# Gates of the last nine blocks of nodes as diagonal matrices on TensorE, and a bias added one stage later

## The chip, the cores and the metric

The kernel runs on one core of one Trainium2 chip. The metric is the device time of one execution in microseconds. Engines are named as the profile names them: PE is TensorE (PEld its weight loads), DVE is VectorE, ACT is ScalarE, POOL is GpSimd and SP is SyncE, which only issues DMAs here.

## The reference

Four layers work on one table of 6250 nodes with 256 features, `x`. Each adds its result to `x`, and each begins with a layer norm of `x` without learned weights. The two in the middle meet in the change:

```python
def _L0_ffn_ref(x, ...):                  # the second layer: attention gates, four experts
    ...
    scores = _layernorm(agg, ln_gamma, ln_beta).reshape(M, HEADS, NUM_EXPERTS).mean(1)
    topk_s, topk_i = jax.lax.top_k(scores, TOP_K)
    w = jax.nn.softmax(topk_s, axis=-1)
    out = jnp.zeros_like(x)
    for ei in range(NUM_EXPERTS):
        g = jnp.where(topk_i == ei, w, 0.0).sum(-1)
        hh = jax.nn.gelu(x @ W1[ei] + b1[ei], approximate=False)
        out = out + g[..., None] * (hh @ W2[ei] + b2[ei])
    return out

def _L1_gnn_ref(x, edge_vals, Wp, bp, W1, b1, W2, b2, src, dst):     # the third layer
    h = jax.nn.relu(x @ Wp.T + bp)
    msgs = edge_vals[:, None] * (h ** 2)[src]
    agg = jax.ops.segment_sum(msgs, dst, num_segments=N) ** 0.5
    return h @ W1.T + b1 + agg @ W2.T + b2

x = x + _L0_ffn_ref(_layernorm(x)[None], ...)[0]
x = x + _L1_gnn_ref(_layernorm(x), edge_weight, ...)
x = x + _L1_ffn_ref(_layernorm(x)[None], ...)[0]
```

So each node's four expert outputs are weighted by the node's own four gates (two of them zero), summed and added to `x`. The third layer adds `b1 + b2`, the same row for every node, to its result.

## The kernel before

**Tiling.** The nodes lie in T = 49 blocks of P = 128 (the last holds 106). `x_all` holds the whole of `x` in SBUF, one block as 128 partitions by 256 elements; `b_all`, of the same shape, holds what the next product reads. Everything is f32.

**The second layer.** Three things run interleaved. POOL gathers edges and the attention sums (`add_up`, `score`, `weigh`, `spread_out`) run over 80 groups. The generator `experts1` (L1571) computes the experts' outputs in units of one expert and two blocks, in batches of eight blocks (the last batch, blocks 40 to 48, has nine; within a batch all units of expert 0 come first, those of expert 3 last). A unit makes `hh` by two products and a Gelu (L1607), then `py` = `hh` times `W2` in PSUM, adds the bias into `ys` (L1623), and SP stores `ys` to `y1_dram` (L1627). The generator `gates` (L1845) turns the attention sums of some blocks into `gate[:, w, e]`, for blocks up to 8, 16, 24, 32, 36, 40, 44 and 49; the last two calls thus cover blocks 40 to 43 and 44 to 48.

**The sums and the table for the next layer.** `load_outputs` (L1934) loads a block's four outputs back from `y1_dram` as soon as all four are stored and a buffer of `y1` is free (eight buffers, two blocks). `node_values` (L1945) takes two blocks at a time (the last pass one, block 48). On DVE it adds the four outputs, each multiplied by its gate, to `x_all` (L1952: `x_all = y * gate + x_all`, the gate one value per partition), and takes mean and variance (L1957 to L1959). ACT makes the square root (L1963), DVE the reciprocal and the offset (L1965, L1966), ACT the normalized block `xn` (L1972), PE transposes it (L1982), ACT copies it into `b_all` (L1983), PE multiplies by `wpt` and ACT applies the bias and Relu (L1989). PE transposes back (L1993), ACT squares into `hp` (L1995), and SP stores `hp` to `hp_dram` (L1996). All these PSUM tiles, and those of the experts' `py`, share one name, `py`, with two buffers.

**The third and fourth layers.** When all 49 blocks of `hp_dram` are stored, POOL gathers rows of it, one instruction (L1104) for 128 edges, 831 in all, four groups of six ahead. For each, DVE makes the weights `eq` (L2390) and PE adds up `pe` (L2411), which first is set to zero by a product with the tile `nothing` (L2406). When a group of blocks is complete (four, two or one block), `roots` (L2419) adds `b12` = `b1 + b2` to these blocks of `x_all` on DVE (L2422) and takes the square root of `pe` on ACT (L2428). `end_of2` then makes for every block the two products with `w1t` and `w2t` in PSUM (`pm`), adds them to `x_all` on DVE (L2229) and begins the last layer norm (L2231 to L2236, L2238 to L2242). The gates and experts of the fourth layer (`gates2`, `experts2`) follow, and the result is stored.

**What sets the order.** Each engine runs its instructions in order. The order on an engine is not that of the text: instructions that depend on little stand earlier. The adds of L2422, in the text behind the first gathers, run from 2456.38, before any gather; the products of L2406 run at 2451.49, ahead of the last transposes of `node_values`.

Of the kernel before, what the change touches and what calls it, by code (L numbers as in the profile page):

```python
# [8 lines left out]
F32 = mybir.dt.float32  # L9
I32 = mybir.dt.int32  # L10
AF = mybir.ActivationFunctionType
OP = mybir.AluOpType
# [4 lines left out]
P = 128  # L17
# [824 lines left out]
def kernel(ctx: ExitStack, tc: tile.TileContext, a: dict, out: bass.AP):  # L842
# [10 lines left out]
    N, D = a["x"].shape  # L853
    T = -(-N // P)
# [23 lines left out]
    H, X = a["L0_ffn_att_src"].shape  # L878
# [21 lines left out]
    V, SC, TE, GP, SY = nc.vector, nc.scalar, nc.tensor, nc.gpsimd, nc.sync  # L900
# [16 lines left out]
    with ExitStack() as fast:  # L917
# [4 lines left out]
        ident = const.tile([P, P], F32, name="ident")  # L922
# [43 lines left out]
        if T1 > C1:  # L966
            V.memset(flat.bitcast(I32)[:, C1:T1], 2**24)
            n = E1 - C1 * P
# [52 lines left out]
        x_all = const.tile([P, T, D], F32, name="x_all")  # L1021
# [66 lines left out]
        def mm(dst, lhs, rhs, n=2):  # L1088

            for c in range(n):  # L1090
                TE.matmul(dst, lhs(c), rhs(c), start=c == 0, stop=c == n - 1)  # L1091
# [91 lines left out]
        gate = att.tile([P, T, X], F32, name="gate")  # L1183
# [96 lines left out]
        with ExitStack() as layer:  # L1280
# [29 lines left out]
            with (  # L1310
# [16 lines left out]
                for t0, t1 in parts0:  # L1327
                    b = t0 // TB
# [5 lines left out]
                    for i in range(t1 - t0):  # L1334
# [4 lines left out]
                            scale=rs[:, i : i + 1],  # L1339
# [224 lines left out]
        psy = experts.enter_context(tc.tile_pool(name="py5", bufs=2, space=PSUM))  # L1564
# [85 lines left out]
        def advance(queue, n):  # L1650
            for _ in range(n):
                if queue and next(queue[0], queue) is queue:
                    queue.pop(0)

        layers = [experts1()]
        part = sums.tile([P, 3, T, H], BF16, name="part")
        with (
# [273 lines left out]
            ys = {}  # L1931
# [13 lines left out]
            def node_values(ws):  # L1945

                mv = n6.tile([P, 2, 2], F32, name="ln_mv")
                rs = n6.tile([P, 2], F32, name="ln_rs")
                off = n6.tile([P, 2], F32, name="off")
                for i, w in enumerate(ws):  # L1950
                    for e in range(X):
                        V.scalar_tensor_tensor(  # L1952
                            x_all[:, w, :], ys.pop((w, e)), gate[:, w, e : e + 1], x_all[:, w, :],
                            op0=OP.mult, op1=OP.add,
                        )
                    st = n6.tile([P, 6], F32, name="ln_st")
                    V.bn_stats(st, x_all[:, w, :])  # L1957
                    V.bn_aggr(mv[:, i, :], st)
                    V.tensor_scalar(rs[:, i : i + 1], mv[:, i, 1:2], EPS, None, op0=OP.add)  # L1959
                    done["sums"] += 1  # L1960
                    yield w == ws[-1]
                n = len(ws)
                SC.activation(rs[:, 0:n], rs[:, 0:n], AF.Sqrt)  # L1963
                yield False
                V.reciprocal(rs[:, 0:n], rs[:, 0:n])  # L1965
                V.scalar_tensor_tensor(  # L1966
                    off[:, 0:n], mv[:, 0:n, 0], -1.0, rs[:, 0:n], op0=OP.mult, op1=OP.mult
                )
                xns = {}
                for i, w in enumerate(ws):  # L1970
                    xns[w] = n6.tile([P, D], F32, name="xn")
                    SC.activation(  # L1972
                        xns[w], x_all[:, w, :], AF.Identity, bias=off[:, i : i + 1],
                        scale=rs[:, i : i + 1],
                    )
                    yield False
                begun.remove(ws)
                for w in ws:
                    pt = psy.tile([P, 2, D], F32, name="py")[:, 0, :]
                    for c in range(2):  # L1980
                        at = slice(c * P, (c + 1) * P)
                        TE.transpose(pt[:, at], xns[w][:, at], ident)  # L1982
                    SC.activation(b_all[:, w, :], pt, AF.Copy)  # L1983
                    yield False
                for w in ws:
                    ph = psy.tile([P, 2, D], F32, name="py")[:, 0, 0:P]
                    mm(ph, lambda c: wpt[:, c, :], lambda c: b_all[:, w, c * P : (c + 1) * P])

                    SC.activation(b_all[:, w, 0:P], ph, AF.Relu, bias=bp)  # L1989
                    yield False  # L1990
                for w in ws:
                    py = psy.tile([P, 2, D], F32, name="py")
                    TE.transpose(py[:, 0, 0:P], b_all[:, w, 0:P], ident)  # L1993
                    hp = n6.tile([P, PD], F32, name="hp")
                    SC.activation(hp, py[:, 0, 0:P], AF.Square)  # L1995
                    SY.dma_start(nodes(hp_dram)[:, w, :], hp)  # L1996
                    yield False
# [157 lines left out]
        blocks = [(t, BT) for t in range(0, small, BT)]  # L2155
        blocks += [(t, 2) for t in range(small, T - 3, 2)] + [(t, 1) for t in range(T - 3, T)]
        with (
# [62 lines left out]
            def end_of2(b, i, root):  # L2220


                w = blocks[b][0] + i
                pm = psm.tile([P, D], F32, name="pt")
                mm(
                    pm, lambda c: (b_all[:, w, 0:P], root[:, i, :])[c],
                    lambda c: (w1t, w2t)[c],
                )
                V.tensor_add(x_all[:, w, :], x_all[:, w, :], pm)  # L2229
                st = wk.tile([P, 6], F32, name="ln_st")  # L2230
                V.bn_stats(st, x_all[:, w, :])  # L2231
                mv = wk.tile([P, 2], F32, name="ln_mv")
                V.bn_aggr(mv, st)
                rs = wk.tile([P, 1], F32, name="ln_rs")
                V.tensor_scalar(rs, mv[:, 1:2], EPS, None, op0=OP.add)
                SC.activation(rs, rs, AF.Sqrt)  # L2236
                yield
                V.reciprocal(rs, rs)  # L2238
                off = wk.tile([P, 1], F32, name="off")
                V.tensor_scalar(off, mv[:, 0:1], rs, -1.0, op0=OP.mult, op1=OP.mult)  # L2240
                xn = wk.tile([P, D], F32, name="xn")
                SC.activation(xn, x_all[:, w, :], AF.Identity, bias=off, scale=rs)  # L2242
                yield
                transposed(psm, b_all[:, w, :], xn)
                yield
                pg = psm.tile([P, D], F32, name="pt")
                mm(pg[:, 0:NX], lambda c: b_all[:, w, c * P : (c + 1) * P], lambda c: gw[:, c, :])
                V.tensor_add(logits(b)[:, i * NX : (i + 1) * NX], pg[:, 0:NX], gb)
# [169 lines left out]

            def roots(b):  # L2419
                n = blocks[b][1]  # L2420
                at = slice(blocks[b][0], blocks[b][0] + n)
                V.tensor_add(  # L2422
                    x_all[:, at, :], x_all[:, at, :],
                    b12[:, None, :].to_broadcast([P, n, D]),
                )
                root = wk.tile([P, BT, P], F32, name="gt")[:, 0:n, :]
                pe = sums.pop(b)[:, 0 : n * P].rearrange("p (w k) -> p w k", k=P)
                SC.activation(root, pe, AF.Sqrt)  # L2428
                return [(b, i, root) for i in range(n)]
# [116 lines left out]
```

## Time and profile before

| What | us |
|---|---|
| median of 3 runs (3552.38 to 3555.68) | 3555.01 |
| the profiled execution, its own time | 3555.79 |
| its span (what the profile covers) | 3554.0 |
| gates of blocks 40 to 43 ready (end of L1921) | 2426.9 |
| gates of blocks 44 to 48 ready (end of L1921) | 2441.1 |
| last store of experts' outputs issued (L1627) | 2444.2 |
| sums and statistics of block 48 done (L1959) | 2454.2 |
| last store to `hp_dram` issued (L1996) | 2464.7 |
| first gather of the third layer (L1104) | 2467.6 |
| last of the 831 gathers starts | 3505.4 |
| last DVE instruction | 3545.3 |

The times below the span count from its start. Over the span PE is busy 94%, DVE 61%, ACT 40% and POOL 63%; these are means over stages with different limits, and the change acts in a short part of one stage and all along another. Two lines show the groups of instructions that the change removes or moves (by their durations; the second line has six smaller ones besides):

```profile
L1952 DVE SCALAR_TENSOR_TENSOR x_all<-y,gate,x_all x196: 446/477/503, 1716.8 to 2452.9; 128x256 f32<-128x256 f32 x196
L2422 DVE TENSOR_TENSOR x_all<-x_all,b 128x1024 f32<-128x1024 f32 x10 | 11.7, 1219 | 0.0
```

The first reads: smallest, median and largest duration in ns, then the starts of the first and the last. The second: total us, mean ns of one, and the idle time of the engine ahead of them. The six smaller ones are 128x512 (three) and 128x256 (three); the six together take 3.3 us.

### The profile page before, as it was taken

Reading aid. Unit: us, or ns where it says so; the run is one execution under the profiler, and the core shown is the slowest. Engines: PE = TensorE matmul, PEld = TensorE weight load, DVE = VectorE, ACT = ScalarE, POOL = GpSimd, SP = SyncE. Lnnn points to the kernel's source line nnn. Section 1 sums busy time; section 2 is a strip of 40 time slices with the busy share of each in tenths; the row PEclk is TensorE's granted clock in tenths of the full one; section 3 lists DMA queues with packets and bytes.
Section 4 is the critical chain, followed back from the end, with each engine's and each line's share of the span. In section 5 each row is a group of like instructions: output and inputs, shape, how many; then the busy total and the mean of one; then the engine's idle time right before and its main releaser. Section 6 shows DMA issues by size and latency. Waiting matters only on the chain.

```text
span 3554.0 us, 57573 instructions
## 1 busy us (share of the span) xinstructions
PE 3338.9 (94%) x20063; PEld 2662.0 (75%) x20063; DVE 2170.1 (61%) x6210; ACT 1412.1 (40%) x2750; POOL 2252.3 (63%) x2367
## 2 busy tenths in 40 slices
PE   7999999999999999999999999997678988989898
PEld 3577777777777778888888888895456666666677
DVE  9999996444544444787758576977234444444464
ACT  4444444444444444444544454664011212211133
POOL 0376666666666664676656555662777777777773
PEclk9999999999999999999999999998567776777797
DMA  6456656656555554433434343553112222222221
GB/s 174 128 189 189 184 183 184 186 186 182 183 183 188 181 183 142 110 97 96 125 88 127 83 130 84 154 94 109 52 53 59 60 59 59 59 59 60 65 62 37
DMA packets 342928, 428.52 MB, mean 121 GB/s; under 512 B 139174, under 2 KB 246453, under 8 KB 342630
## 3 DMA queue, kind: packets, MB, share of 16 engines
q1 hardware_dynamic: 245174, 244.98, 22.1%
q0 software_dynamic: 89408, 178.08, 19.4%
q8 instruction: 162, 2.65, 0.3%
q10 hardware_dynamic: 8048, 1.68, 0.2%
q14 instruction: 136, 1.11, 0.1%
HBM read 382.05 MB, written 42.49 MB: 119 GB/s over the span
## 4 chain that ended last, share of the span: by engine, by line
PE 66%; POOL 14%; DMA 7%; issue 7%; DVE 4%; ACT 1%; SPq 0%; ACTq 0%; POOLq 0%; DVEq 0%
PE ph L1091 32%; POOL hg L1104 13%; PE py L1091 10%; PE pt L1085 7%; PE pe L1443 6%; PE po L1771 5%; DMA hg<-hp_dram,src 5%; PE pt L1091 2%; DMA rb<-low_dram 1%; PE pe L2411 1%; PE pa L1708 1%; PE pm L1091 1%; DVE junk L982 1%; DVE key L1240 0%; DVE order L1237 0%
## 5 line engine op out<-in xcount | busy, mean ns | idle before, releaser
L1104 POOL DMA_INDIRECT yg<-y_dram,src x882 | 847.0, 960 | 543.1 <-issue 226.7
L1104 POOL DMA_INDIRECT hg<-hp_dram,src x831 | 785.7, 946 | 269.2 <-issue 224.3
L1104 POOL DMA_INDIRECT sg<-gat_dram,src x640 | 614.1, 960 | 350.1 <-issue 161.5
L1091 PE MATMUL ph<-w1b,et 128*128 128x256 f32 x3528 | 835.7, 380 | 0.0
L1091 PEld LDWEIGHTS ph<-w1b,et 128*128 128x128 f32 x3528 | 637.0, 190 | 68.7
L2411 PE MATMUL pe<-eq,hg 128*128 128x96 f32 (+15 forms) x2036 | 439.9, 353 | 148.9 <-DMA hg<-hp_dram,src 120.6
L2411 PEld LDWEIGHTS pe<-eq,hg 128*128 128x128 f32 x2036 | 388.2, 260 | 251.8 <-issue 94.6
L1417 DVE TENSOR_TENSOR yg<-ph,yg 128x512 f32<-128x512 f32 x441 | 303.3, 688 | 375.3 <-PE ph L1091 370.7
L2390 DVE TENSOR_SCALAR eq<-px,dst,ew 128x96 f32<-128x96 f32 x831 | 262.0, 370 | 217.2 <-PE pe L2411 120.6
L1091 PE MATMUL ph<-b_all,w 128*128 128x256 f32 (+1 forms) x1600 | 387.1, 380 | 1.5 <-ACT hh L1607 1.4
L1091 PE MATMUL py<-w,hh 128*128 128x256 f32 x1568 | 383.1, 384 | 5.0 <-ACT hh L1607 4.5
L1086 ACT ACTIVATE et<-pt 128x512 f32<-128x512 f32 x441 | 262.2, 596 | 254.4 <-PE pt L1085 242.1
L1422 ACT ACTIVATE h<-yg 128x512 f32<-128x512 f32 x441 | 276.1, 626 | 215.4 <-DVE yg L1417 209.0
L1091 PEld LDWEIGHTS py<-w,hh 128*128 128x128 f32 x1568 | 288.7, 190 | 41.2 <-ACT hh L1607 6.6
L1091 PEld LDWEIGHTS ph<-b_all,w 128*128 128x128 f32 x1600 | 290.0, 190 | 33.7 <-ACT hh L1607 2.0
L1607 ACT ACTIVATE hh<-ph,b 128x256 f32<-128x256 f32 (+1 forms) x400 | 166.7, 467 | 285.6 <-PE ph L1091 279.7
L1085 PE MATMUL pt<-ident,ea 128*128 128x128 f32 x1764 | 272.1, 277 | 3.4 <-ACT et L1086 3.4
L1085 PEld LDWEIGHTS pt<-ident,ea 128*128 128x128 f32 x1764 | 210.2, 144 | 65.0 <-issue 40.4
L1771 PE MATMUL po<-pp,B 128*128 128x240 f32 (+10 forms) x1280 | 252.1, 337 | 2.2 <-DVE acc L1777 2.1
L1771 PEld LDWEIGHTS po<-pp,B 128*128 128x128 f32 x1280 | 215.6, 190 | 14.3 <-DVE acc L1777 2.8
L1443 PE MATMUL pe<-h,eq 128*32 128x257 f32 x3168 | 216.8, 384 | 3.7 <-ACT h L1422 1.9
L1443 PEld LDWEIGHTS pe<-h,eq 128*32 128x32 f32 x3168 | 96.2, 109 | 102.6 <-issue 35.0
(330 smaller groups left out, 4264.5 us busy)
## 6 DMA issues: line engine op xcount, KB each, us to landing
ea<-in_edge_attr_dram SPq DMA_DIRECT2D x147, 768.0 KB
y<-y SPq DMA_DIRECT2D x196, 128.0 KB
w<-in_L_ffn_W_dram SPq DMA_DIRECT2D x48, 512.0 KB
y<-ys SPq DMA_DIRECT2D x96, 256.0 KB
rb<-low_dram SPq DMA_DIRECT2D x80, 256.0 KB
yg<-y_dram,src POOLq DMA_INDIRECT x882
hg<-hp_dram,src POOLq DMA_INDIRECT x831
sg<-gat_dram,src POOLq DMA_INDIRECT x640
```

The source lines that it names most:

```text
L982: V.tensor_scalar(junk, flat, float(w * P), None, op0=OP.is_lt, op1=OP.add, accum_out=below[:, w : w + 1],)
L1085: TE.transpose(pt[:, c, :], src[:, c * P : (c + 1) * P], ident)
L1086: SC.activation(dst, pt.rearrange("p c k -> p (c k)"), AF.Copy)
L1091: TE.matmul(dst, lhs(c), rhs(c), start=c == 0, stop=c == n - 1)
L1104: GP.indirect_dma_start(out=dst, out_offset=None, in_=table[0:NP, :], in_offset=IndirectOffsetOnAxis(ap=idx, axis=0),)
L1417: V.tensor_add(y, ph, y)
L1422: SC.activation(h[:, j : j + 2, 0:D], y, AF.Relu)
L1443: TE.matmul(sums[w][b * Q : (b + 1) * Q, :], eq[k][:, j, at], h[:, i * NT + j, :], start=g == 0 and j == NT - 1, stop=g == last_of[b] and ...
L1607: SC.activation(hidden[u][:, f, :n, :], ph[:, f - f0, :n, :], AF.Gelu, bias=b1[:, e, f : f + 1],)
L1771: TE.matmul(po.rearrange("p b v -> p (b v)"), B[:, j, :], pp[:, j, 0:n, :].rearrange("p b v -> p (b v)"), start=half == 0 and j == 0, stop ...
L2390: V.tensor_scalar(equals[k][:, j, :], lanes[:, 0:NW], dst_of[:, t : t + 1], ew[:, t : t + 1], op0=OP.is_equal, op1=OP.mult,)
L2411: TE.matmul(sums[b][:, lo - t0 * P : hi - t0 * P], hg[:, j, :], eq[:, j, lo - n0 : hi - n0], start=False, stop=after >= (t0 + n) * P,)
```

## The change

For the last nine blocks (40 to 48) the four products on DVE go. Instead ACT multiplies the identity matrix by a block's gates, one expert at a time, which gives four diagonal matrices of 128x128 in a new tile `dg` (one buffer, 2 KB in each partition); PE multiplies each diagonal by the expert's output and sums the four in a PSUM tile of the name `py`; DVE adds that sum to `x_all`. Blocks 0 to 39 stay as they are.

The add of `b12` goes from `roots`, where one instruction covered up to four blocks, to `end_of2`, where one instruction per block follows the add of `pm`.

```diff
+        LATER = T - 9
...
                 for i, w in enumerate(ws):
-                    for e in range(X):
-                        V.scalar_tensor_tensor(
-                            x_all[:, w, :], ys.pop((w, e)), gate[:, w, e : e + 1], x_all[:, w, :],
-                            op0=OP.mult, op1=OP.add,
-                        )
+                    if w < LATER:
+                        for e in range(X):
+                            V.scalar_tensor_tensor(
+                                x_all[:, w, :], ys.pop((w, e)), gate[:, w, e : e + 1],
+                                x_all[:, w, :], op0=OP.mult, op1=OP.add,
+                            )
+                    else:
+
+                        dg = n6.tile([P, X, P], F32, name="dg", bufs=1)
+                        for e in range(X):
+                            SC.activation(dg[:, e, :], ident, AF.Copy, scale=gate[:, w, e : e + 1])
+                        py = psy.tile([P, 2, D], F32, name="py")[:, 0, :]
+                        mm(py, lambda e: dg[:, e, :], lambda e: ys.pop((w, e)), X)
+                        V.tensor_add(x_all[:, w, :], x_all[:, w, :], py)
...
                 V.tensor_add(x_all[:, w, :], x_all[:, w, :], pm)
+                V.tensor_add(x_all[:, w, :], x_all[:, w, :], b12)
                 st = wk.tile([P, 6], F32, name="ln_st")
...
             def roots(b):
                 n = blocks[b][1]
-                at = slice(blocks[b][0], blocks[b][0] + n)
-                V.tensor_add(
-                    x_all[:, at, :], x_all[:, at, :],
-                    b12[:, None, :].to_broadcast([P, n, D]),
-                )
```

## The prediction

> **What bounds the kernel now.** I read the chain of work that ended last, then the stretch around the change in slices of 5 us, then the instructions of single engines there. In the chain two lines matter, the gathers of the last stage and what stands ahead of the first of them:
>
> ```profile
> 2464.16 0.43 SPq L2187
> 2464.69 0.45 SPq L1996
> 2465.18 2.47 DMA eb<-in_L_ffn_eb_dram
> 2467.65 0.93 POOL hg L1104
> ```
>
> The first gather of `hg` waits until the table `hp_dram` is whole; its last part is stored at 2464.69 (L1996). From there POOL issues 831 gathers at a fixed pace:
>
> ```profile
> L1104 POOL DMA_INDIRECT hg<-hp_dram,src x831: 940/944/1546, 2467.6 to 3505.4; - x167
>   issue: 224.3, 736
>   DMA hg<-hp_dram,src: 22.5, 74
> ```
>
> (3505.4 − 2467.6) / 830 = 1.25 us each, and none of the listed idle times is over 0.3 us but the first. So POOL carries the last stage, and the change can act in two places only: before 2467.6, by the time at which `hp_dram` is whole, and after 3506.3, in the 47.7 us of rest. The stretch before it (columns: span, then busy us of PE, PEld, DVE, ACT, POOL; granted clock):
>
> ```profile
> 2430.00:2435.00 5.00, 1.92 (x15) 1.53 (x14) 5.00 (x24) 4.83 (x10) 0.00 (x0) 1.00 0.76 245
> 2435.00:2440.00 5.00, 4.56 (x24) 3.91 (x24) 4.72 (x24) 4.67 (x10) 0.00 (x0) 1.00 0.48 156
> 2440.00:2445.00 5.00, 3.76 (x19) 2.76 (x20) 4.19 (x15) 2.74 (x8) 0.00 (x0) 1.00 0.36 118
> 2445.00:2450.00 5.00, 1.64 (x10) 1.07 (x10) 4.77 (x20) 2.80 (x7) 2.70 (x2) 1.00 0.75 236
> 2450.00:2455.00 5.00, 3.52 (x7) 1.93 (x8) 3.96 (x15) 2.27 (x6) 1.37 (x2) 0.56 0.68 197
> ```
>
> DVE is full throughout; ACT is full only to 2440. On DVE the end of that stretch reads:
>
> ```profile
> 2452.33 1.00 DVE L1952 SCALAR_TENSOR_TENSOR x_all<-y,gate,x_all 128x256 f32<-128x256 f32 x2
> 2454.05 0.15 DVE L1959 TENSOR_SCALAR ln_rs<-ln_mv 128x1 f32<-128x1 f32 x1
> 2455.92 0.42 DVE L2171 TENSOR_TENSOR b<-b,b 128x256 f32<-128x256 f32 x1 [1.72 <-DMA b<-in_L_gnn_b_dram]
> 2456.38 1.23 DVE L2422 TENSOR_TENSOR x_all<-x_all,b 128x1024 f32<-128x1024 f32 x1
> 2457.53 0.15 DVE L1965 RECIPROCAL ln_rs<-ln_rs 128x1 f32<-128x1 f32 x1
> 2457.60 1.21 DVE L2422 TENSOR_TENSOR x_all<-x_all,b 128x1024 f32<-128x1024 f32 x1
> 2458.72 0.15 DVE L1966 SCALAR_TENSOR_TENSOR off<-ln_mv,ln_rs 128x1 f32<-128x1 f32 x1
> ```
>
> The bias adds of `roots` (L2422) have been put far ahead of their place in the text, between the two small steps of block 48's layer norm.
>
> **The change part by part.** I work against the profiled execution: span 3554.0, its time 3555.79, so 1.8 us lie around the span; the median of the three runs shown, 3555.01, is 0.8 below it.
>
> *DVE, gates.* Removed: 9 x 4 products of L1952 at 0.477 us; eight in a row take 3.26, so one more costs 0.40, 14.4 in all. Added: 9 adds of a PSUM tile, 128x256; nearest row L2229, 0.42. A block now costs DVE 4 x 0.40 + 0.42 + 0.17 + 0.15 (L1957 to L1959) = 2.34, and five blocks (44 to 48) 11.7; measured, with other work between them, 2441.16 to 2454.20 = 13.0. After: 0.42 + 0.74 = 1.16 a block, 5.8 for five. DVE stops being the bound.
>
> *ACT, diagonals.* 36 activations 128x128 from SBUF with a scale per partition; no such row. From below L1995 (0.275, no operand per partition), from above L1972 (0.595, twice the width, two operands). I take L1989's 0.368 (same size, one operand). Four of L1607 at twice the width take 1.58 at 0.475 each, so the next starts 0.10 before the one before it ends; a block is 0.37 + 3 x 0.27 = 1.18, nine 10.6 (bounds 7 to 21). No table load: L1983, the same function, runs between Gelu and Sqrt without one.
>
> *TensorE.* 36 products 128x256; eight of `py` take 1.89, so four 0.95, and double that at clock 0.5. One buffer for `dg`: the next block's activations wait for this block's last product, so a block takes 1.18 + 0.24 + hops of some 0.2 = 1.6, five 8.1 against DVE's 13.0.
>
> *What is late next.* Block 48's outputs come from the last unit of `experts1`: stored at 2444.19 (L1627). A store lands about 2.2 after its issue (2444.66 to 2446.84 for `hp_dram`), the four loads take 1.86 to issue and 2.3 to land, so they are there at 2450.6; product, add and statistics (0.25 + 0.1 + 0.42 + 0.74) give 2452.1. The best gain of the sums is 2454.2 − 2452.1 = 2.1, not the 5 that DVE alone would allow. Against it: the 16 activations of blocks 40 to 43 (4.7) fall where ACT is full. ACT idles 2.6 before 2429.90; the other 2.1 push the Gelus at 2434.41 and 2436.07, which the last unit needs, and four more tiles go through `py`'s two PSUM buffers, for which the last unit waits already (0.65 before 2441.44). So between +2.1 and −2.1 x 2 = −4.2 (the second for the PSUM buffers); near the upper end, since the products of 40 and 41 fit the idle: **1.3 gained**.
>
> *Bias, out of `roots`.* The two adds ahead of L1965 and L1966 cost block 48 1.15 + 1.04 = 2.2 on DVE. Its activation L1972 then waited for ACT's place behind L1989 until 2460.38, though `off` was ready at 2458.87; without the adds it could have been at 2456.6. Bounds 0 and 2.2; **1.5 gained**. The eight later adds hide behind the store and its landing: the first product of the last stage waits 5.2 us for `hg`, not for DVE.
>
> *Bias, into `end_of2`.* 49 adds of 0.42 = 20.6 us DVE. Up to 3505 they hide behind the gathers (DVE is under half busy there); were that cover gone, 20.6 minus the 15.0 of L2422. In the rest three blocks remain; for block 48 the statistics are done at 3523.47 and ACT takes up its square root at 3525.58 after a table load, so 0.42 fits there. Bounds 0 and 3 x 0.45 = 1.4; **0.4 lost**.
>
> *Orders.* SP issues small bias loads ahead of the last store (L2186 and L2187, 0.43 each): up to 0.7 better, or some three loads, 1.3, worse. PE waits 4.7 for the memset of `nothing` and runs four products of L2406 (4.0) in front of the transposes of blocks 44 to 47, which were ready at 2451.2 and start at 2453.35: between 2.2 better and as much worse. No POOL or DMA instruction is added or moved in the text; the loads of `y1` only free their buffers later, by PE's last product. I take 0 for both.
>
> The Trainium skill speaks against the first part: "ScalarE: Activation LUTs", section "Rules for kernel authors", has multiplications on VectorE, not ScalarE. By that rule alone the nine blocks would lose; the trace has DVE full and ACT half free from 2440, so I go by the rows.
>
> Sum: −1.3 − 1.5 + 0.4 = −2.4, span 3551.6, and from the median 3555.0 − 2.4 = **3552.6**.
>
> **The rivals.**
> *A, the drain opens wider.* All at the good ends: 2.1 + 2.2 + 0.7 + 2.2 = 7.2 less, 3547.8, and further if the Gelus come forward too: PE idles 3.36 before 2435.31 for `xn` of block 40, which waited for DVE; half of it makes 3546.1. For it: DVE's load. Against: the last unit's store isn't moved by DVE in any other row.
> *B, ACT becomes the bound: slower.* Place: ACT's queue from 2430. Price: the last unit's outputs 4.2 later, and behind the single `dg` buffer ACT stands still for five blocks' products (5 x 0.4 = 2.0), with copies and layer norms of earlier blocks queued behind it. That is 4.2 + 2.0 + 0.4 − 2.2 (the bias at its best) = +4.4 and 3559.4; without the bias's gain +6.6, 3561.6. It decides from the point where the last unit's store comes over 2.1 after 2444.19, since then nothing of the gain of the sums is left.
> *C, hidden anyway.* The store comes when the other blocks' steps on ACT and PE let it, and both edits cancel: −0.4 to +0.4, 3555.0.
>
> **How the numbers follow.** Forecast (3549 to 3554.5) 0.44, A 0.21, B 0.18, C 0.17. What a measurement of this kernel can tell from no change is about 0.2%, 7.1 us: faster than 3547.9 in most of A and a little of the forecast, 0.17; slower than 3562.1 only in the far part of B, 0.07; the rest, 0.76. The range takes A to its worked end and most of B: 3546 to 3560.
>
> **What would show it.** Right: DVE no longer full in 2430 to 2454; L1627's last store near 2444; L2422 gone ahead of L1965; the last store of L1996 at about 2461.9; gathers at 1.25; the rest about 48. Wrong: the last Gelu past 2438 (B); ACT waiting for PE at the new activations; gathers that wait for anything; a rest of over 49.5.

## The result, and the profile after

The changed kernel took 3577.55 us (median of four executions, 3573.81 to 3584.47), the kernel before 3555.35 beside it (four, 3552.38 to 3559.82): a ratio of 1.0063, 95% interval 1.0051 to 1.0075. It is slower by some 22 us, where 2.4 less were forecast, and lies above the range. The profiled execution took 3573.81, its span is 3572.0, 18.0 more than before.

| What | before | after | difference |
|---|---|---|---|
| gates of blocks 44 to 48 ready | 2441.1 | 2440.2 | −0.9 |
| last Gelu of `experts1` starts (L1607) | 2436.07 | 2441.89 | +5.8 |
| last store of experts' outputs issued (L1627) | 2444.19 | 2446.73 | +2.5 |
| sum of block 48 in `x_all` | 2453.3 | 2468.5 | +15.2 |
| last store to `hp_dram` issued (L1996, now L2007) | 2464.69 | 2474.62 | +9.9 |
| first gather | 2467.6 | 2476.9 | +9.3 |
| last of the 831 gathers starts | 3505.4 | 3514.3 | +8.9 |
| from there to the end of the span | 48.6 | 57.7 | +9.1 |

So the loss comes in two halves: 9.3 in the drain of the second layer ahead of the first gather, and 9.1 in the tail behind the last. Between them nothing changed.

The profiles don't all reach the drain at the same time: in kernels that up to there have the text of the kernel before, the gates of blocks 44 to 48 are ready anywhere from 2438.8 to 2445.0. So the drain is better measured from those gates to the first gather: 26.5 before and 36.7 after, 10.2 more. The tables below give both.

The gathers' own group in the changed kernel (smallest, median, largest ns; first and last start; then idle time ahead of them):

```profile
L1104 POOL DMA_INDIRECT hg<-hp_dram,src x831: 940/944/1181, 2476.9 to 3514.3; - x167
...
  issue: 235.0, 771
  DMA hp_dram<-hp: 24.0, 1
```

The pace is still (3514.3 − 2476.9) / 830 = 1.25. The drain in slices (busy us of PE, PEld, DVE, ACT, POOL; then the granted clock):

```profile
2430.00:2435.00 5.00, 5.00 (x29) 4.50 (x28) 3.03 (x14) 4.92 (x12) 0.00 (x0) 1.00 0.34 101
2435.00:2440.00 5.00, 5.00 (x25) 4.08 (x23) 0.97 (x5) 4.92 (x8) 0.00 (x0) 1.00 0.27 91
2440.00:2445.00 5.00, 4.35 (x22) 3.38 (x21) 2.57 (x10) 3.97 (x14) 0.00 (x0) 1.00 0.66 207
2445.00:2450.00 5.00, 3.64 (x18) 2.58 (x17) 0.66 (x3) 3.51 (x8) 1.20 (x1) 1.00 0.22 71
2450.00:2455.00 5.00, 4.88 (x25) 3.53 (x23) 2.53 (x9) 3.38 (x13) 2.87 (x3) 1.00 0.72 219
```

DVE is no longer full, as meant; PE, which had 1.92 and 1.64 of 5 in two of these slices, is now the fullest engine. What it does from there, in its own order (the last bracket is PE's idle time and who ended it):

```profile
2447.66 0.93 PE L1993 MATMUL py<-ident,xn 128*128 128x128 f32 x4 [1.31 <-ACT xn L1983]
...
2448.57 1.99 PE L1091 MATMUL py<-y,dg 128*128 128x256 f32 x8
...
2451.12 1.99 PE L1091 MATMUL py<-y,dg 128*128 128x256 f32 x8
...
2455.85 0.93 PE L1993 MATMUL py<-ident,xn 128*128 128x128 f32 x4 [0.36 <-ACT xn L1983]
...
2456.76 1.99 PE L1091 MATMUL py<-y,dg 128*128 128x256 f32 x8
...
2460.58 1.97 PE L1091 MATMUL py<-y,dg 128*128 128x256 f32 x8 [1.38 <-ACT dg L1963]
...
2465.19 0.93 PE L1993 MATMUL py<-ident,xn 128*128 128x128 f32 x4 [1.28 <-ACT xn L1983]
2466.10 1.99 PE L1091 MATMUL py<-y,dg 128*128 128x256 f32 x8
```

Two things are to be read here. The sum of one block is eight records, 1.99, not 0.95. And the sums stand behind the transposes of the pair before (L1993), which wait for `xn`: blocks 44 and 45, then transposes, 46 and 47, then transposes, 48. From the first sum's start to the last add it takes 2468.55 − 2448.57 = 20.0 for five blocks, 4.0 a block; on DVE it was 2441.16 to 2453.3, 12.1 or 2.4 a block.

The tail, in slices of 10 us, first of the kernel before, then of the changed kernel 10 us later, and PE's wait for the normalized block 48 in each:

```profile
3520.00:3530.00 10.00, 8.94 (x55) 6.80 (x54) 5.25 (x26) 7.99 (x18) 0.00 (x0) 1.00 0.05 15
3530.00:3540.00 10.00, 9.98 (x60) 7.53 (x58) 7.04 (x37) 5.16 (x17) 0.00 (x0) 1.00 0.04 13
...
3528.07 0.44 PE L1085 MATMUL pt<-ident,xn 128*128 128x128 f32 x2 [0.83 <-ACT xn L2242]
```

```profile
3530.00:3540.00 10.00, 6.08 (x36) 4.59 (x34) 5.00 (x22) 7.15 (x15) 0.00 (x0) 1.00 0.04 13
3540.00:3550.00 10.00, 9.93 (x33) 6.88 (x33) 3.79 (x22) 3.16 (x11) 0.00 (x0) 0.51 0.01 2
3550.00:3560.00 10.00, 9.99 (x49) 7.92 (x48) 4.39 (x21) 4.37 (x14) 0.00 (x0) 0.81 0.04 13
...
3540.07 0.57 PE L1085 MATMUL pt<-ident,xn 128*128 128x128 f32 x2 [2.77 <-ACT xn L2254]
```

PE stands still for 2.77 instead of 0.83, and is then granted half its clock: the slice is full with 33 instructions where the one before the change held 60. In slices of 2 us the clock reads 0.56 at 3540, 0.50 from 3542 to 3552 and 0.53 at 3552, which is 0.9 + 5.0 + 0.9 = 6.8 us of full-speed work lost. With the longer wait, 1.9, that is 8.7 of the 9.1. This sum is an estimate; it leaves out a later wait of PE for DVE of 1.76, ahead of its last product, which the kernel before doesn't have.

### The profile page after: what moved, and what is told of

The parts are those of the page before. It is cut to its first block, busy times and chain, and to the rows that moved or that the text cites. A ratio compares the mean times of both kernels' runs of the same rounds, so it can differ in the third digit from the quotient of the medians.

```text
span 3572.0 us, 57761 instructions
## 1 busy us (share of the span) xinstructions
PE 3351.5 (94%) x20135; PEld 2667.8 (75%) x20135; DVE 2162.9 (61%) x6216; ACT 1425.6 (40%) x2788; POOL 2252.6 (63%) x2367
## 4 chain that ended last, share of the span: by engine, by line
PE 67%; POOL 13%; issue 8%; DMA 5%; DVE 4%; ACT 1%; SPq 1%; ACTq 0%; POOLq 0%; DVEq 0%
PE ph L1091 32%; POOL hg L1104 13%; PE py L1091 11%; PE pt L1085 7%; PE pe L1443 6%; PE po L1773 5%; DMA hg<-hp_dram,src 3%; PE pt L1091 3%; PE pe L2423 2%; DMA rb<-low_dram 1%; PE pa L1710 1%; DVE junk L982 1%; DVE key L1240 0%; DVE order L1237 0%; DVE ln_st L1062 0%
## 5 line engine op out<-in xcount | busy, mean ns | idle before, releaser
L1607 ACT ACTIVATE hh<-ph,b 128x256 f32<-128x256 f32 (+1 forms) x400 | 166.4, 466 | 280.4 <-PE ph L1091 274.8
```

The source lines that it names most:

```text
L1607: SC.activation(hidden[u][:, f, :n, :], ph[:, f - f0, :n, :], AF.Gelu, bias=b1[:, e, f : f + 1],)
```

## The experiments

The theory after this comparison: **Q** for the drain (the sums stand in PE's queue behind the transposes of the pair before, and each is twice as long as costed); for the tail, the add behind the product, later **O** and **C**: the order of the last blocks, and the clock behind the wait. Rivals for the drain: the single buffer of `dg`, the two PSUM buffers of `py`, and DVE's wait of 4.56 for the row of `b2` (L2182), which holds up the add of block 46. "First gather", "from the gates" (the same, counted from the end of the gates of blocks 44 to 48) and "rest" (from the last gather's start to the end of the span) are read from each profile; before they are 2467.6, 26.5 and 48.6, after 2476.9, 36.7 and 57.7.

**Four first runs: each edit alone, and the two buffers.** They ran at a time when the kernel before itself took 4359.52, for a reason that the record doesn't show. So only their ratios are read, and distances within the drain and the tail.

```diff
 e1_diag_only, from the changed kernel: the bias back into roots
-                V.tensor_add(x_all[:, w, :], x_all[:, w, :], b12)
 e2_bias_only, from the kernel before: the bias into end_of2, behind the product
+                V.tensor_add(x_all[:, w, :], x_all[:, w, :], b12)
 e3_dg_halves, from the changed kernel
-                        dg = n6.tile([P, X, P], F32, name="dg", bufs=1)
+                        for h in range(2):
+                            dg = n6.tile([P, 2, P], F32, name="dg", bufs=2)
 e4_ph_psum, from the changed kernel
-                        py = psy.tile([P, 2, D], F32, name="py")[:, 0, :]
+                        py = psh.tile([P, 2, 2, P], F32, name="ph")
```

> Diagonals for blocks 40 to 48 as in the changed kernel, the bias added in roots as before. The changed kernel lost 9.3 us before the first gather (2467.6 to 2476.9) and 9.1 us behind the last (48.6 to 57.7 after its start). Theory 1: the two losses belong to the two edits, the first to the diagonals. Then the first gather starts near 2477 (2475 to 2479), the rest stays near 48.6, and the time is some 9 us over before, 3564. Rival: both come from the diagonals (what follows is only shifted by them, and the clock falls in the rest whatever the bias does): rest 55 to 58, time near 3577. Second rival: without the bias adds gone from its way the drain is worse still, first gather 2479 or later.

> The products of the gates on DVE as before for all blocks, the bias added in end_of2 as in the changed kernel. Theory 1: the first gather starts 0 to 2.2 us earlier than before (2465.4 to 2467.6), since the adds ahead of block 48's offset are gone, and the rest behind the last gather's start grows from 48.6 to near 57.7, so that the time is 7 to 9 us over before, 3563. Rival: the rest grows only by the adds themselves, 0.4 to 1.4 us, and the time is 3554 to 3556.

> The changed kernel with its diagonals in two tiles of two, each with its own buffer, so that a block's first two activations need only the first two products of the block before. ACT waited 7.5 us for PE at the activations between 2425 and 2500. If the single buffer causes the loss, these waits fall by half or more and the first gather comes 3 to 5 us earlier than 2476.9 (2472 to 2474). If the order of PE's queue causes it (the sums of a pair stand behind the transposes of the pair before), the waits may fall but the first gather moves by less than 1.5 us.

> The changed kernel with the sums of the nine blocks in the PSUM tiles of the experts' first products (two further buffers) instead of those of py. If the two buffers of py, which transposes, products and sums share, set the order in which a pair follows the other, the sums of blocks 46 to 48 no longer stand behind the transposes of the pair before, and the first gather comes 4 us or more earlier than 2476.9 (2470 to 2473). If not, it moves by less than 1.5 us.

Ratios to the kernel before: 1.0034 (1.0008 to 1.0061), 1.0032 (1.0001 to 1.0064), 1.0077 (1.0043 to 1.0111) and 1.0060 (1.0029 to 1.0092). Each edit alone costs about half of the whole. For the buffers these intervals are too wide: they reach some 14 us to either side, and a gain of 3 to 5 was asked for. The traces say more. From the gates it is 43.8 with the diagonals alone, 25.7 with the bias alone and 35.8 with `dg` in halves, so a second buffer of `dg` gives back 0.9 of the 10.2. With the sums in the `ph` tiles the gates themselves come earlier in the order; counted from the gates of blocks 40 to 43 the first gather comes 50.5 later, against 52.3 with the whole change: 1.8 back. Neither buffer is the main cause.

**Each edit alone again, and two orders.** The third puts the bias of a block ahead of the product instead of behind it; the fourth lets the next pair of blocks begin its sums right behind this pair's.

```diff
 f3_bias_ahead, from the kernel before: out of roots, and in end_of2
+                V.tensor_add(x_all[:, w, :], x_all[:, w, :], b12)
                 pm = psm.tile([P, D], F32, name="pt")
 f4_diag_early, from f1_diag_again, in node_values
+                begun.remove(ws)
                 n = len(ws)
                 SC.activation(rs[:, 0:n], rs[:, 0:n], AF.Sqrt)
...
-                begun.remove(ws)
```

> Only the gates as diagonals; the bias stays in roots. Theory Q (the sums stand in PE's queue behind the transposes of the pair before, and the bias is the loss of the tail alone): the first gather of hg late as in the changed kernel, 2474 to 2478 (2467.64 before, 2476.91 with the whole change), and behind the last gather's start 47 to 50 as before (48.6): 7 to 11 us over the kernel before, ratio 1.002 to 1.003. Rival (the two edits disturb each other, as the last diagonals delay the bias row and DVE waits 4.56 for it): the first gather below 2472.

> Only the bias: out of roots, added in end_of2 behind the product's add. Theory Q: the first gather at 2464 to 2469 as before, and behind the last gather's start 55 to 60 (48.6 before, 57.7 with the whole change): 6 to 11 us over the kernel before, ratio 1.002 to 1.003. Rival (the tail is late because the whole change's first gather is late, so that the last blocks crowd): rest 47 to 50, ratio 0.999 to 1.000. The forecast's own term would be 1.1 us faster.

> The kernel before with the bias out of roots and added in end_of2 ahead of the product, so that nothing behind the product waits for it, and the order of the tail stays that of the kernel before except for these adds. Theory Q (the add behind the product lengthens the chain of each block's layer norm and changes the order on DVE): rest 47 to 50, ratio 0.9985 to 1.0005 if the adds find room in the drain. Rival (the 49 adds of some 0.37 move up into the drain, where DVE is full): the first gather 3 to 10 later, 2470 to 2478, ratio 1.001 to 1.003. Rival (any bias add per block costs the tail): rest 55 to 60.

> Only the diagonals, and a pair of blocks gives the next pair leave right behind its sums instead of behind its normalized values, so that the next pair's sums stand ahead of this pair's transposes on PE; the same instructions in another order. Theory Q: the first gather comes back by 4 us or more, to 2466 to 2473, ratio 0.9995 to 1.0012. Rivals (the one buffer of the diagonals, for which ACT waits 7.5 in the whole change, or the products of 1.99 a block): 2474 to 2478 as with the diagonals alone, ratio 1.002 to 1.003.

| run | ratio, 95% interval | first gather | from the gates | rest |
|---|---|---|---|---|
| diagonals alone | 1.0044, 1.0027 to 1.0060 | 2485.1 | 44.3 | 45.8 |
| bias alone, behind the product | 1.0030, 1.0019 to 1.0041 | 2466.4 | 25.3 | 57.8 |
| bias alone, ahead of it | 1.0006, 0.9996 to 1.0016 | 2465.9 | 25.7 | 47.4 |
| diagonals alone, pairs early | 1.0045, 1.0029 to 1.0062 | 2482.8 | 43.5 | 46.8 |

The split is clean: the diagonals lose in the drain alone, the bias in the tail alone. But the diagonals alone are worse there than the whole change, by 8.2 or, from the gates, by 7.6, and that was not expected (2474 to 2478 was). Letting the pairs in early, Q's own remedy, was expected to bring the first gather back to 2466 to 2473, and gives back 0.8. DVE's order shows why:

```profile
2465.19 0.42 DVE L1968 BATCH_NORM_STATS2 ln_st<-x_all 128x6 f32<-128x256 f32 x1
2465.53 1.21 DVE L2433 TENSOR_TENSOR x_all<-x_all,b 128x1024 f32<-128x1024 f32 x1
2466.65 0.18 DVE L1969 BATCH_NORM_AGGREGATE ln_mv<-ln_st 128x2 f32<-128x6 f32 x1
2466.74 1.20 DVE L2433 TENSOR_TENSOR x_all<-x_all,b 128x1024 f32<-128x1024 f32 x1
2467.85 0.15 DVE L1970 TENSOR_SCALAR ln_rs<-ln_mv 128x1 f32<-128x1 f32 x1
2467.92 1.22 DVE L2433 TENSOR_TENSOR x_all<-x_all,b 128x1024 f32<-128x1024 f32 x1
```

The big adds of `roots`, which before stood behind all sums but two steps of block 48, now stand between the small steps of each block, since DVE's order leaves gaps there for PE's sums. So in the whole change the bias's move saved 7.6 of what the diagonals cost.

**What in the tail.** The bias behind the product for the last three blocks only, for all others only, and for block 48 only; elsewhere in `roots`, as before. The fourth is the whole change with the pairs early.

```diff
 t1_last_three, t2_all_but_three, t3_block_48: late = b >= len(blocks) - 3; b < len(blocks) - 3; b == len(blocks) - 1
                 V.tensor_add(x_all[:, w, :], x_all[:, w, :], pm)
+                if late:
+                    V.tensor_add(x_all[:, w, :], x_all[:, w, :], b12)
 h1_after_early, from the changed kernel: the edit of f4_diag_early
```

> The kernel before with the bias of the last three blocks, 46 to 48, added behind the product in end_of2, and that of all others in roots as before. Theory O (the add puts the normalization of block 47 behind the experts of block 46 in the order on ACT and DVE, so that PE runs dry and is then granted half the clock): behind the last gather's start 55 to 60 as with the bias of all blocks (57.8), 48.6 before; ratio 1.002 to 1.003. Rival L (three adds of 0.42 lengthen the chain, and nothing else): 49 to 50.5, ratio 1.0000 to 1.0007. Rival S (the sum of 49 adds on DVE through the gathers): 48 to 50.

> The complement: the bias of all blocks but the last three behind the product in end_of2, that of blocks 46 to 48 in roots. Theory O: behind the last gather's start 47 to 50, first gather 2464 to 2469, ratio 0.999 to 1.0005. Rival S (the many adds): 55 to 60, ratio 1.002 to 1.003.

> Only block 48, the very last, has its bias behind the product; the order on ACT and DVE at the end stays that of the kernel before but for a swap of neighbours. Theory O: the price of the add itself, 0.3 to 0.9 behind the last gather's start (48.9 to 49.5), time within 0.05% of before. Rival (an add on the last chain costs several times its length): 52 or more.

> The whole change, and a pair of blocks lets the next pair in right behind its sums instead of behind its normalized values, so that the next pair's sums stand ahead of this pair's transposes on PE. Theory Q (the sums wait in PE's queue behind the transposes of the pair before): first gather 2468 to 2474 (2476.91 with the whole change), 3 to 9 us below the whole change, ratio to before 1.004 to 1.0055; the tail stays at 55 to 60. Rivals (the one buffer of the diagonals, or the length of the products and diagonals themselves): first gather 2475 to 2479, ratio 1.0055 to 1.0075.

| run | ratio, 95% interval | first gather | from the gates | rest |
|---|---|---|---|---|
| blocks 46 to 48 | 1.0031, 1.0020 to 1.0041 | 2467.6 | 25.5 | 55.1 |
| blocks 0 to 45 | 1.0000, 0.9990 to 1.0009 | 2465.1 | 25.7 | 47.5 |
| block 48 | 1.0013, 1.0003 to 1.0023 | 2465.5 | 26.7 | 55.3 |
| whole change, pairs early | 1.0061, 1.0045 to 1.0078 | 2479.5 | 38.2 | 57.5 |

The last three blocks make the loss of the tail (6.5 in the profiled execution, and the ratio of all blocks together), and the other 46 none. Block 48's single add of 0.42 was expected to cost 0.3 to 0.9 and cost 6.7 in the profiled execution. The run with block 48 alone shows how (PE's wait and the slices of 10 us):

```profile
3526.58 0.44 PE L1085 MATMUL pt<-ident,xn 128*128 128x128 f32 x2 [1.99 <-ACT xn L2244]
...
3520.00:3530.00 10.00, 7.93 (x45) 6.74 (x44) 5.90 (x31) 6.24 (x14) 0.00 (x0) 0.86 0.05 15
3530.00:3540.00 10.00, 10.00 (x31) 6.83 (x31) 3.54 (x18) 2.67 (x10) 0.00 (x0) 0.50 0.00 0
```

The wait grew from 0.83 to 1.99, and the clock fell as in the changed kernel. The statistics of block 48 were done in time (3521.70; ACT took up the square root's table load only at 3523.05), so the add itself did fit. But one Relu of the experts had moved ahead of the square root in ACT's order, and PE had done its products before it came to wait. The ten times of this kernel lie between 3552.92 and 3563.95, three of them below 3555: it seems to stand on the edge. This run also separates the clock from the wait. From the start of block 48's transposes to the end of the span, in the kernel before and then in this one:

```profile
3528.06:3554.00 25.94, 15.77 (x90) 11.59 (x90) 11.52 (x60) 8.03 (x26) 0.00 (x0) 0.85 0.06 18
3526.57:3559.80 33.23, 23.23 (x90) 17.46 (x90) 11.52 (x60) 8.15 (x26) 0.00 (x0) 0.61 0.03 10
```

The counts of instructions left are the same on every engine, and the transposes even start a little earlier behind the last gather's start (22.1, before 22.7). What follows takes 7.3 longer, with PE busy 7.5 longer at the lower clock. So here the clock is the whole loss.

In the whole change too, letting the pairs in early failed: 2479.5 where 2468 to 2474 was expected.

**The clock, and the suspects of the drain.** The first kernel is the bias alone behind the product, with six spare products whose result nothing reads, ahead of block 48's transposes. The next two take suspects of the drain away: `b2` is neither loaded nor added; then that, the pairs early and `dg` in halves together. The fourth uses diagonals only for blocks 40 to 43.

```diff
 c1_bridge, from e2_bias_only, in end_of2 behind the square root
+                if w == T - 1:
+                    spare = psy.tile([P, 2, D], F32, name="py")
+                    for _ in range(6):
+                        TE.matmul(spare[:, 0, :], x_all[:, w, 0:P], x_all[:, w, :], start=True, stop=True)
 k1_no_b2, from the changed kernel (k2_no_b2_early_halves: with the edits of e3 and f4 as well)
-            V.tensor_add(b12, b12, bcast_row(wp, "b2", a["L1_gnn_b2"]))
 h2_after_40_43, from the changed kernel
-                    if w < LATER:
+                    if w < LATER or w > LATER + 3:
```

> The bias behind the product for all blocks, as in the run with the bias alone (behind the last gather's start 57.8, granted clock 0.50 after PE's wait of 2.77 for xn of block 48), and six spare products 128x256 on block 48's values ahead of that block's transposes, whose result nothing reads: some 3.7 of added work at full clock. Theory C (the wait makes the granted clock halve for some 13 us, and that is most of the loss): the wait falls below 1, the clock stays at 0.9 or over to the end of PE's work, and the rest is 49 to 54, ratio 0.9995 to 1.0018, in spite of the added work. Rival O (the order and the waits themselves are the loss, the clock a bystander): rest 58 to 62, ratio 1.003 or more.

> The whole change without b2: its row is neither loaded nor added to the bias (the output lacks it). Theory S (DVE waits 4.56 for that row and holds up the add of block 46, and PE behind it): first gather 2472 to 2475.5 (2476.91 with the whole change), tail 55 to 60, ratio 1.0045 to 1.0058. Rival (the wait lies beside the chain of the pairs): first gather 2476 to 2479, ratio 1.0057 to 1.0075.

> The whole change with all three suspects of the drain away: no b2, the next pair let in right behind the sums, and the diagonals in two tiles of two with a buffer each. Theory QDS (they hide each other: with one away, the next takes its place; letting the pair in early alone gave 2479.5): first gather 2466 to 2472, tail 55 to 60, ratio 1.003 to 1.0045. Rival W (the work itself, 1.2 of diagonals on ACT and 1.99 of products on PE for each block in the chain of outputs, sums and normalization): first gather 2474 to 2479, ratio 1.005 to 1.007.

> The whole change with the diagonals only for blocks 40 to 43; 44 to 48 are summed on DVE as before. Theory W or QDS (the loss of the drain is made by blocks 44 to 48, whose sums stand in PE's queue and take longer there): first gather 2464 to 2470, tail 55 to 60, ratio 1.0015 to 1.0035. Rival (the loss is made by 40 to 43, whose products push the last experts back by 2.5): first gather 2470 to 2478, ratio 1.0035 to 1.006.

| run | ratio, 95% interval | first gather | from the gates | rest |
|---|---|---|---|---|
| bias behind the product, spare products | 1.0010, 1.0000 to 1.0020 | 2467.3 | 25.8 | 52.3 |
| whole change without `b2` | 1.0062, 1.0045 to 1.0078 | 2478.4 | 36.7 | 57.6 |
| without `b2`, early, halves | 1.0061, 1.0045 to 1.0078 | 2478.2 | 37.2 | 59.8 |
| whole change, diagonals for 40 to 43 | 1.0033, 1.0022 to 1.0045 | 2469.4 | 27.4 | 60.1 |

With the spare products in (L2242; block 48's transposes behind them), the kernel is faster than without them, 1.0010 against 1.0030:

```profile
3525.83 2.76 PE L2242 MATMUL py<-x_all 128*128 128x256 f32 x12
...
3529.29 0.38 PE L1085 MATMUL pt<-ident,xn 128*128 128x128 f32 x2
...
3520.00:3530.00 10.00, 8.69 (x49) 7.26 (x50) 4.45 (x24) 6.69 (x16) 0.00 (x0) 1.00 0.01 2
3530.00:3540.00 10.00, 9.04 (x55) 7.09 (x54) 5.92 (x27) 5.28 (x15) 0.00 (x0) 1.00 0.04 13
```

PE does 2.76 of useless work where it had waited 2.77, block 48's transposes start without a wait, and the clock stays at 1.00. The rest is 52.3: the 47.5 of the undisturbed tail, the 2.8, and 2.0 more. So 5.5 of the 57.8 with the bias alone come back, though the wait is filled with work of no use. Up to 1.9 of this may be due to the order instead: block 48's `xn` starts 23.0 behind the last gather here, and 24.8 with the bias alone. (Two of the experts' products also stand ahead of the transposes here; they take 1.0, and alone could not fill the wait.) With the run of block 48 alone this shows that the halved clock behind PE's wait makes the larger part of the 9.1.

In the drain, counted from the gates, the diagonals of blocks 44 to 48 make 36.7 − 27.4 = 9.3 of the 10.2 (7.5 of the 9.3 by the times of the first gather). Of the suspects none stands: `b2`'s wait away gives nothing, and all three away give nothing, as the rival W of that run (the work itself in the chain) had it. Without `b2` the sum of block 47 does start without a wait, 1.3 earlier in the chain, but there the clock was at 0.50 from 2466.9, and the sum of block 48 took 3.31 instead of 1.99:

```profile
2460.84 1.99 PE L1091 MATMUL py<-y,dg 128*128 128x256 f32 x8
...
2466.37 3.31 PE L1091 MATMUL py<-y,dg 128*128 128x256 f32 x8
```

The trace of the kernel with all three away shows the late work changing places. Its sums of 44 to 48 run in 2454.48 to 2468.0, 2.7 a block instead of 4.0. But the sums of 42 and 43 now stand among the last experts' products, and the queue then waits for the memset of `nothing`:

```profile
2453.49 0.42 DVE L1623 TENSOR_TENSOR ys<-py,b 128x256 f32<-128x256 f32 x1
...
2461.19 1.12 PE L2421 MATMUL pe<-nothing,ident 128*128 128x512 f32 x2 [1.62 <-POOL nothing L2232]
```

The last unit's outputs leave DVE from 2453.49, where in the changed kernel it was 2446.28, and the sum of 44 begins 5.9 later than there. PE also ran at a clock of 0.50 from 2445.3 to 2452.1, behind two waits of 0.78 and 1.53.

**A version that shares the sums.** Diagonals for 45 and 47 only, so that PE sums the second block of a pair while DVE sums the first; the bias as in `t2_all_but_three`. The second kernel lets the pairs in early as well.

```diff
 m1_45_47 (m2_45_47_early: with the edit of f4 as well), from the changed kernel
-                    if w < LATER:
+                    if w not in (T - 4, T - 2):
```

> A version that keeps what the runs left standing: the bias of blocks 46 to 48 in roots, that of the others behind the product (first gather 2465.1, rest 47.5 and ratio 1.000 with that alone), and diagonals for blocks 45 and 47 only, so that PE sums the second block of a pair while DVE sums the first. Theory P (the engines share the sums: DVE is spared two blocks of 2.34, PE gets two of 1.99 where it has idle time): first gather 2461 to 2465, ratio 0.998 to 1.000. Rival (any sum in PE's queue stands behind the transposes of the pair before and comes later than on DVE): first gather 2466 to 2470, ratio 1.000 to 1.002.

> The same, and a pair lets the next in right behind its sums, so that on PE the sum of 47 stands ahead of most transposes of 44 and 45. Theory P: first gather 2459 to 2464, ratio 0.997 to 0.9995. Rival (the transposes then wait for the sum, as all of it goes through PE): first gather 2465 to 2470, ratio 1.000 to 1.002.

Ratios 1.0016 (1.0007 to 1.0025) and 1.0012 (1.0003 to 1.0021), first gather 2476.2 and 2475.9, rest 49.5 and 48.4. Theory P failed. The first gather looks as late as with nine sums on PE, but both profiles reach the gates of blocks 44 to 48 only at 2444.9. From there it takes 31.3 and 30.9, which is 5.6 and 5.2 more than in `t2_all_but_three`, with the same bias and all sums on DVE. So each of the two sums costs 2.6 to 2.8, and each of the five of blocks 44 to 48 cost 1.9. In the first of these kernels PE runs the products of `nothing` 10.4 behind the gates, as in the kernel before, but all four of them at once and mostly at half the clock:

```profile
2455.30 3.58 PE L2419 MATMUL pe<-nothing,ident 128*128 128x512 f32 x4 [2.86 <-POOL nothing L2229]
```

These records stand ahead of the transposes of 44 and 45 and of the sum of 47 in PE's order, and so 47 is summed at 2462.1, 17.2 behind the gates, where DVE had even 48 done 12.2 behind them. No version that I tried beats the kernel before; the bias moved ahead of the product, or behind it for all but three blocks, equals it.

## Why the prediction was wrong, and where it was right

**What bounds.** Right: the gathers pace the last stage at 1.25, and the change acted only ahead of the first and behind the last.

**TensorE: "eight of `py` take 1.89, so four 0.95".** Wrong, by a factor of two. Eight records are four products: the 36 products leave 72 records, and a block's four take 1.99.

```profile
L1091 PE MATMUL py<-y,dg x72: 379/379/483, 2425.1 to 2467.7; 128*128 128x256 f32 x72
L1963 ACT ACTIVATE dg<-ident,gate x36: 384/388/403, 2424.6 to 2464.2; 128x128 f32<-128x128 f32 x36
```

The row to count by was in the kernel before: one block's `py` from four parts of `hh` was x8 as well. The activations were costed right, 0.388 against 0.368, four in 1.27 against 1.18.

**"So a block takes 1.6, five 8.1", and "what is late next".** This is the step that lost the drain. Measured: 4.0 a block and 20.0 for five, against 12.1 on DVE. Of the 12 over the forecast, some 5 are the products' true length (an estimate, 5 x 1.04). The rest is what PE's queue holds between the sums: transposes with their waits of 0.36 and 1.28, the products of `wpt`, the four products of `nothing`, and a wait of 1.38 ahead of the sum of block 47. The profile puts that one down to the diagonals, but the first of them was done at 2459.2; what ended just before was the add of block 46 (2460.5), which frees a `py` buffer and stood behind DVE's wait for `b2`. I asked only when the last unit's outputs come (forecast near 2444, measured 2446.73), not what stands ahead of the sums on the engine that they move to. On DVE they stood ahead of the normalization of their own pair and ran on while PE and ACT worked at the pair before; on PE they stand behind it. That the sums of blocks 44 to 48 on PE make 9.3 of the 10.2 is shown. How much of it is the length of the work and how much the order on PE is read from the traces alone: each remedy of the order gave back at most 1.8, some moved the late work to another place, and every sum moved cost 1.9 to 2.8 wherever it stood, which speaks for the length.

**The rivals.** B came nearest: the last Gelu is past 2438, and its point of decision, a last store over 2.1 later, was passed with 2.5. ACT did stand still for PE's products, 7.5 in all, but a second buffer gave back only 0.9. Nor do the late outputs make the loss: with the diagonals for 40 to 43 alone they are as late (21.7 behind the gates of 40 to 43, as in the changed kernel; 16.6 before), and from the gates of 44 to 48 the first gather is 0.9 later. ACT was busy 3.5 of 5 us or less from 2445, PE more, and B's +4.4 to +6.6 held only half of the loss of the drain. The rule in "ScalarE: Activation LUTs", section "Rules for kernel authors", by which the multiplications stay on VectorE, would have given the right sign; the trace doesn't show its reason, as ACT wasn't what ran late.

**"Bias, out of `roots`": 1.5 gained.** Inside its bounds, but its cause isn't shown. From the gates the first gather comes 1.2 earlier with the bias alone, and 0.8 in the two variants that cost nothing in the tail. Yet `t1_last_three`, which keeps the two big adds between block 48's steps, has it 1.0 earlier as well. In company of the diagonals the move is worth 7.6, since without it the adds of `roots` fall among the last blocks' steps; the forecast didn't have that.

**"Bias, into `end_of2`": 0.4 lost, "0.42 fits there".** The term that lost the tail, 9.1. The add of block 48 did fit ahead of the square root (statistics done at 3536.10, ACT free for it at 3536.55). What failed is that I priced a step of 0.42 and not the wait that it lengthens. Block 48's normalization was waited for by PE, for 0.83; when the wait had grown to 1.99 or 2.77, the granted clock was halved behind it for over 10 us.

**Orders, taken as 0.** Wrong where it mattered. The same add for blocks 0 to 45 costs nothing, for 46 to 48 all; the order of the last blocks on ACT and PE, and so PE's wait, is what it changes.

**Readings.** Three of the forecast's readings were off, without effect on its sum that a run shows: DVE was not full throughout 2430 to 2455 but 0.79 to 1.00 busy; the transposes at 2453.35 are those of 44 and 45 alone; PE's wait before 2441.44 is 0.41, not 0.65.

## What to carry to other kernels

Work moved to an engine with idle time can still lengthen the chain, by its own length there and by what stands ahead of it in that engine's order: list the instructions between which it will stand, and what each of them waits for. When two profiles are compared, count from a point that both reach by the same work, not from the start of the span. Count products by their records in a row whose number of products is known. Where a busy PE comes to a short wait near the end, cost what lengthens that wait at the clock it may lose, and see in the runs whether some spare products in the wait are cheaper.

## What the runs showed of the hardware

The granted clock was either 1.00 or 0.50. In these traces it fell behind PE waits of 1.99, 2.77, 2.86 and 4.66, and behind 0.78 and 1.53 close together. It stayed at 1.00 behind single waits of 0.83, 1.15, 1.38 and 1.62. A wait of 3.36 for the first `xn` of the drain stands in nine of these kernels, those outside the first four runs in which DVE sums blocks 40 to 43. The kernel before (at 2435.31) and `m2_45_47_early` kept 1.00 there; the seven others had 0.50 during it or within 1.3 us of its end. And in the kernel before the clock fell at 2464.3, behind waits of 0.48, 0.33, 0.41 and 0.53 within 4 us. So the length of one wait doesn't decide alone.

The stretches at 0.50 last 3.4 us or close to a whole multiple of it: 3.4 in `m1_45_47` (2455.6 to 2459.0), 6.8 in the kernel before (2450.6 to 2457.4) and in `k2_no_b2_early_halves`, 13.7 in the changed kernel's tail (3540.2 to 3553.9) and 17.1 in the run with block 48's bias (3527.2 to 3544.3). PE was busy almost without a gap in all of these but the first us of some. What decides the number is not known.

The Trainium skill, "TensorE: Matmul & The Clock Gate", section "Part 1: The HAM clock gate (the "warmup" mystery)", tells of half the clock after an idle window of some 3.4 us that runs free of the kernel, and of full clock after as long a busy one. Stretches in steps of 3.4 us, and one wait of 3.36 with two outcomes, agree with a window that runs free. That waits of 1.99 sufficed, and that four and five such windows with PE busy were needed in the tails, are not what it states.
